# Paired Gelus, a period of three slots and weighted turns in a convolution and attention kernel

## The chip, the cores and the metric

The kernel runs on one NeuronCore of one Trainium2 chip. The metric is the device time of one execution in microseconds (us), as the median of several runs. Engines are named TensorE (PE in the profile, PEld for its weight loads), VectorE (DVE), ScalarE (ACT), GpSimd (POOL) and SyncE (SP, which issues the DMAs here).

## The reference

Four layers work on four images of 128 channels and 64 x 64 pixels in fp32. Layers 0 and 1 are where the change lies:

```python
# layer 0, on group-normalised x
feat = _gelu(_dwconv2d(x_adapted, conv1_w, conv1_b))
ca = feat.mean((2, 3))
ca = jax.nn.sigmoid(jnp.maximum(ca @ ca1_w.T, 0.0) @ ca2_w.T)
feat = feat * ca[:, :, None, None]
feat = _gelu(_dwconv2d(feat, conv2_w, conv2_b))
scores = jax.nn.sigmoid(jnp.einsum('bchw,oc->bohw', feat, head_w)[:, 0] + head_b[0])
pv = jnp.var(x_adapted, axis=1, ddof=1)
final_scores = 0.7 * scores + 0.3 * jax.nn.sigmoid(pv * 10.0)
sm = final_scores.reshape(B, Hp, PS, Wp, PS).mean((2, 4)).reshape(B, Hp * Wp)
idx = jnp.argsort(-sm, axis=1)
...
h = dA_t * h + dBx_t                      # a scan over 4096 positions, 256 x 16 states
...
# layer 1
x = x + _L1_conv_ref(_gn(x), L1_conv_weight, L1_conv_bias)      # a 3 x 3 convolution, 128 to 128 channels
```

In words: layer 0 scores the 4 x 4 patches of an image by two depthwise convolutions with exact Gelus and by the variance over channels, sorts the patches by score, sends the sorted pixels through a selective state-space scan and puts the result back in the old order. Layer 1 is a dense 3 x 3 convolution. Layer 2 is an attention with softmax and a mixture of experts, layer 3 a linear attention and another mixture. Layers 2 and 3 are not touched.

## The kernel before, in words

**Stages.** `layers01` has three stages. First `in_order(0)` prepares image 0 alone: group norm, first depthwise convolution, channel weights, second depthwise convolution with scores, sort, position encoding and layer norm, permutation. Then `scan` runs the state-space scans of the four images, one after the other, with other work beside them: `in_order(b + 1)` while image b is scanned, and, beside the last scan (image 3), `end` of images 2, 0 and 1, which puts sorted pixels back (`put_back`) and runs layer 1 (`convolve`). Last comes `end(3)` alone. Layers 2 and 3 follow.

**Chunks and slots.** An image of 4096 positions is cut in 8 chunks (`NCH`) of 512 (`CH`). For a chunk the scan has 8 state groups (`NG`) of four scans each; a group is two slots, so a chunk has 16 slots (`SLOTS`), a scan of an image 128. I count the slots of an image from 0 to 127: slot 66 is slot 2 of chunk 4. At the head of a group VectorE multiplies into `hs` (line 901); each slot then has two exponentials on ScalarE (line 908, "decay", in two PSUM banks), a flush of the work put off, two scans on VectorE (line 912), a carry copy and a product with the C row on GpSimd (lines 915 and 916). In odd slots TensorE adds the previous group into `y_ps` (`add`); in even slots, after the work beside it, it spreads the next B row (`b_ps`, `spread_b`), and SyncE loads the next C row (`c_sb`, `spread_c`). In the first slots of a chunk `enter` prepares the next chunk (`xc_ps`, Silu, `dbc`, `dt`), and `leave` finishes the last one. `gate` comes in slot 8.

**The order of the work.** In the scan stage all five engines run in the order in which the code issues (`tc.manual_schedule`); alone, before and after it, a scheduler may reorder. The work beside the scans consists of generators; one `next` is a turn. Beside scans 0 to 2 one turn is taken per slot, and all that is left in slot 111; beside scan 3 turns are taken from slot 8 at an even pace, 53 turns an end (`TURNS_END`), 159 turns in 120 slots. `staged(n, period, ...)` starts item c at turn c x period and runs one stage a turn; `together` and `chain` combine generators. The second depthwise convolution of chunk c is issued in slot 47 + 2c, the first one's in slot 27 + 2c.

What reads a result of TensorE is put off: `K.later` keeps it for the next `K.flush`, which is called in each slot between the exponentials and the scans, and between two turns of one slot. `K.bank` hands out the three PSUM banks that the work beside shares; when the bank due is still in use, it flushes at once:

```python
while self.count - self.banks in self.live:
    assert self.late
    self.flush()
```

`enter` holds a bank from slot 1 of a chunk until its Silus are issued, in the flush of slot 3 or in an earlier one that `K.bank` forces.

**What the change touches.** `first` (line 476) and `second` (line 530) are the depthwise convolutions of one chunk, `gauged` (line 539) sums squares and features over channels and takes a Tanh; `seconds` (line 557) schedules them. Before, Gelu reads PSUM for each chunk, adds the bias and, in `first`, accumulates the sum for the channel weights. Gelu and Exp need different activation tables, so that a Gelu beside the scans has a table load ahead of it and one behind. `put_back`, `convolve` and `end` (lines 955 to 1029) are the last stage's turns; `Common.__init__` and `same_block` make constants.

## Time and profile before

| what | value |
|---|---|
| median of 3 runs | 9885.43 us (9885.13 to 9886.97) |
| the profiled execution, its own time | 9881.09 us |
| its span, first to last instruction | 9879.3 us |
| mean granted clock of TensorE | 0.92 |
| preparation of image 0 and first entry | 0 to 236.8 us |
| scan of image 0, 1, 2 | 580.1, 582.0, 579.8 us |
| scan of image 3, with three ends | 656 us |
| end of image 3, alone | to some 2750 us |
| busy in scans 0 to 2, each | VectorE 509 to 511, TensorE 478 to 481, ScalarE 398 to 399, GpSimd 417 to 422 us |

How to read the page: busy time is the sum over an engine's instructions; the lines of tenths cut the span in 40 slices. In a list of groups the columns are line, engine, operation, tiles written and read, count, then busy us and mean ns, then the idle time of the engine just ahead of these instructions, with what ended it. In a timeline they are start, duration, engine, line, instruction, and in brackets the idle time before it and its releaser. Helpers hide lines: all matmuls through `mm` stand at line 91, all that is put off by `K.later` with its arguments at line 130.

### The profile page before, as it was taken

What the parts mean: (1) busy time and instruction counts of PE and PEld (TensorE: products, weight loads), DVE (VectorE), ACT (ScalarE), POOL (GpSimd) and SP (SyncE); (2) the same over time, 40 slices, a digit from 0 to 9 for tenths busy, and PEclk for the clock granted to TensorE, in tenths of its full rate; (3) what the DMA queues carried; (4) which work ended last, traced back from release to release, by engine and by line L of the source; (5) the groups of instructions that cost most, each with busy time, mean ns of one, the idle gap of its engine ahead of it and who ended that gap; (6) DMA issues with size and microseconds to landing.
All of it is one profiled execution on the core that took longest, in us unless ns stands there. A gap on an engine that the chain in (4) does not pass through costs nothing.

```text
span 9879.3 us, 187787 instructions
## 1 busy us (share of the span) xinstructions
PE 8736.1 (88%) x74074; PEld 3348.6 (34%) x74074; DVE 7220.5 (73%) x7877; ACT 7410.6 (75%) x10669; POOL 4802.8 (49%) x3175
## 2 busy tenths in 40 slices
PE   5888888888869999989999989999989999967776
PEld 2222222244523333333333333333333333333433
DVE  2889897988658888758888758888758888743463
ACT  3766767654359999879999879999879999841531
POOL 1677676765435555455555455555455555420000
PEclk8887878889979999989999989999989999988997
DMA  4524435223121221231111131211131211124004
GB/s 116 124 69 118 97 83 125 67 76 88 46 70 40 40 40 41 48 94 39 40 39 41 46 97 39 40 40 39 44 101 39 39 40 39 40 93 121 1 18 154
DMA packets 575731, 635.31 MB, mean 64 GB/s; under 512 B 113080, under 2 KB 369152, under 8 KB 573824
## 3 DMA queue, kind: packets, MB, share of 16 engines
q1 hardware_dynamic: 574848, 623.30, 25.6%
q8 instruction: 584, 9.57, 0.4%
q14 instruction: 299, 2.45, 0.1%
HBM read 446.84 MB, written 109.07 MB: 56 GB/s over the span
## 4 chain that ended last, share of the span: by engine, by line
PE 69%; DVE 10%; POOL 6%; ACT 5%; DMA 4%; issue 3%; SPq 2%; DVEq 0%; POOLq 0%; ACTq 0%
PE ctx_ps L91 27%; PE acc_ps L91 13%; PE score L91 11%; PE conv L91 4%; DVE hs L912 3%; POOL hs L916 3%; PE ln_xc L91 2%; PE y_ps L91 2%; DVE hs L901 2%; PE xc_ps L91 1%; DMA w<-in_L_ffn_weight 1%; PE ln_var L91 1%; PE b_ps L91 1%; PE hid_ps L91 1%; PE kv L91 1%
## 5 line engine op out<-in xcount | busy, mean ns | idle before, releaser
L1535 ACT ACTIVATE ex<-score 128x1024 f32<-128x1024 f32 x5120 | 4925.4, 1036 | 218.5 <-PE score L91 125.7
L91 PE MATMUL ctx_ps<-ex,qt 128*32 128x512 f32 x20480 | 2733.9, 606 | 19.9 <-DVE ctx L1469 19.9
L1484 POOL TENSOR_TENSOR folded<-ex 128x1024 f32<-128x1024 f32 x512 | 1224.2, 2391 | 2101.5 <-ACT ex L1535 1836.6
L1541 DVE STREAM_TRANSPOSE turned<-ex 128x1024 f32<-128x1024 f32 x1536 | 1885.8, 1228 | 329.1 <-ACT ex L1535 328.7
L1517 DVE STREAM_TRANSPOSE turned<-ex 128x1024 f32<-128x1024 f32 x1532 | 1842.4, 1203 | 0.0
L91 PE MATMUL acc_ps<-turned,turned_v 128*32 128x256 f32 x24576 | 1769.5, 379 | 3.1 <-POOL qt L1229 2.3
L912 DVE TENSOR_TENSOR_SCAN hs<-decay,carry,hs 128x512 f32<-128x512 f32 x1024 | 1245.7, 1266 | 193.6 <-ACT decay L908 180.1
L91 PE MATMUL score<-queries,keys 32*128 32x512 f32 x10240 | 1335.3, 497 | 44.0 <-POOL queries L1219 37.9
L91 PEld LDWEIGHTS acc_ps<-turned,turned_v 128*32 128x32 f32 x24576 | 800.9, 110 | 1476.5 <-issue 1323.8
L916 POOL TENSOR_TENSOR hs<-hs,c_sb 128x1024 f32<-128x1024 f32 x512 | 1207.3, 2358 | 81.4 <-DMA c_sb<-c_d 40.3
L908 ACT ACTIVATE decay<-dt,a_neg 128x512 f32<-128x512 f32 x1024 | 693.0, 689 | 662.5 <-DVE hs L912 653.3
L91 PEld LDWEIGHTS score<-queries,keys 32*128 32x128 f32 x10240 | 512.6, 182 | 1139.2 <-ACT ex L1535 780.9
L1347 POOL TENSOR_TENSOR turned_v<-v,quarter 128x1024 f32<-128x1024 f32 x256 | 612.4, 2393 | 265.7 <-PE acc_ps L91 225.0
L91 PE MATMUL y_ps<-hs,pair 128*64 128x512 f32 x2048 | 661.5, 773 | 33.6 <-POOL hs L916 33.6
L1485 POOL TENSOR_TENSOR quarters<-folded 128x512 f32<-128x512 f32 x512 | 657.7, 1285 | 40.2
L91 PEld LDWEIGHTS ctx_ps<-ex,qt 128*32 128x32 f32 x20480 | 406.4, 108 | 654.7 <-issue 598.7
L901 DVE TENSOR_TENSOR hs<-dtx,b_ps 128x2048 f32<-128x2048 f32 x256 | 580.1, 2266 | 55.9 <-PE b_ps L91 31.6
L91 PE MATMUL b_ps<-dbc,state 32*64 32x512 f32 x1024 | 343.2, 752 | 233.4 <-DVE hs L901 233.2
L1535 ACT ACTIVATION_READ_ACCUMULATOR ex<-score 128x1 f32 x2048 | 435.9, 213 | 0.0
L915 POOL COPY carry<-hs 128x2 f32<-128x2 f32 x512 | 98.1, 192 | 673.4 <-DVE hs L912 652.0
L1469 DVE COPY ctx<-ctx_ps 128x512 f32<-128x512 f32 x256 | 176.9, 691 | 329.3 <-PE ctx_ps L91 327.0
L1526 DVE TENSOR_REDUCE dacc<-quarters 128x2 f32<-128x512 f32 x508 | 327.1, 644 | 0.0
(371 smaller groups left out, 9016.1 us busy)
## 6 DMA issues: line engine op xcount, KB each, us to landing
c_sb<-c_d SPq DMA_DIRECT2D x512, 128.0 KB
queries<-head_d SPq DMA_DIRECT2D x1024, 64.0 KB
keys<-head_d SPq DMA_DIRECT2D x1024, 64.0 KB
under<-image_d SPq DMA_DIRECT2D x192, 264.0 KB
dt<-dt SPq DMA_DIRECT2D x128, 256.0 KB
dtx<-dtx SPq DMA_DIRECT2D x128, 256.0 KB
v<-value_d SPq DMA_DIRECT2D x1024, 32.0 KB
w<-in_L_ffn_weight SPq DMA_DIRECT2D x32, 1024.0 KB
```

Source lines behind the costliest of these rows:

```text
L91: self.nc.tensor.matmul(out, lhsT, rhs, start=start, stop=stop)
L901: nc.vector.tensor_tensor(hs, dtx2, bb.unsqueeze(1).to_broadcast([P, NQ, CH]), ALU.mult)
L908: nc.scalar.activation(ex, dt2[:, q, :], AF.Exp, scale=a_neg[:, q, g : g + 1])
L912: nc.vector.tensor_tensor_scan(hs[:, q, :], decays[q - 2 * i], hs[:, q, :], carry[:, g, q : q + 1], ALU.mult, ALU.add)
L916: nc.gpsimd.tensor_tensor(hs[:, two, :], hs[:, two, :], cs.unsqueeze(1).to_broadcast([P, 2, CH]), ALU.mult)
L1347: nc.gpsimd.tensor_tensor(t, v.unsqueeze(2).to_broadcast([P, 4 * BT, 4, HD]), quarter.unsqueeze(1).to_broadcast([P, 4 * BT, 4, HD]), ALU.mult,
L1484: nc.gpsimd.tensor_tensor(hs, exs[:, :, 0], exs[:, :, 1], ALU.add)
L1485: nc.gpsimd.tensor_tensor(qs, hs[:, :, 0 : CH // 2], hs[:, :, CH // 2 :], ALU.add)
L1517: nc.vector.transpose(*upright)
L1526: nc.vector.tensor_reduce(at, qs, AX.X, ALU.add)
L1535: nc.scalar.activation(ex, sps[p], AF.Exp, scale=scale, accum_out=sums[:, t : t + 1] if summed else None)
L1541: nc.vector.transpose(*upright)
```

## The change

In `first`, ScalarE takes the convolution out of PSUM with an Identity that adds the bias, chunk by chunk, and after every second chunk runs one Gelu in place over both, with one accumulated sum. `second` does the same in a buffer of two chunks, and Squares go to a buffer of two. The scores of both chunks of a pair are then taken in two turns of the later one (`gauged_first`, `gauged_second`), and a chunk of the second convolution begins every three turns instead of two. Chunk c's second convolution is then issued in slot 47 + 3c, the pairs' Gelus come in the flushes of slots 51, 57, 63 and 69, and what follows is seven turns later.

Beside the last scan a turn may carry a weight. The turns of group norm and the waits weigh 0.4, those of `put_back` 0.85, those of `convolve` 0.9, and turns are taken until their weights, not their number, reach what is due; an end counts as 40.3 (`SLOTS_END`).

To make room for the larger buffers, constants that are needed only to make others lie in a pool that is closed again, and two tiles of `put_back` share the place of tiles of the sort.

```diff
-        self.same4 = self.same_block("same4", 2)
-        self.same16 = self.same_block("same16", 4)
-        self.group_mean = pool.tile([P, P], F32, name="group_mean")
-        nc.vector.tensor_scalar(self.group_mean, self.same4, 0.25, None, ALU.mult)
+        with tc.tile_pool(reuse_waits="tile", name="temporary", bufs=1) as tmp:
+            self.same4 = self.same_block("same4", 2, tmp, tmp)
+            self.same16 = self.same_block("same16", 4, tmp, pool)
+            self.group_mean = pool.tile([P, P], F32, name="group_mean")
+            nc.vector.tensor_scalar(self.group_mean, self.same4, 0.25, None, ALU.mult)
...
-    TURNS_END = 53
+    SLOTS_END = 40.3
...
+        def weighted(weight, part):
+
+            while True:
+                try:
+                    next(part)
+                except StopIteration as over:
+                    return over.value
+                yield weight
...
-            fsum = small.tile([P, NCH], F32, name="fsum")
+            fsum = small.tile([P, NCH // 2], F32, name="fsum")
...
-                later(
-                    nc.scalar.activation,
-                    fp[:, 1 + 8 * c : 9 + 8 * c, 1 : HW + 1],
-                    rect(ps),
-                    AF.Gelu,
-                    bias=conv1_b,
-                    accum_out=fsum[:, c : c + 1],
-                )
+                later(nc.scalar.activation, fp[:, 1 + 8 * c : 9 + 8 * c, 1 : HW + 1], rect(ps), AF.Identity, bias=conv1_b)
+                if c % 2:
+                    at = fp[:, 8 * c - 7 : 8 * c + 9, 1 : HW + 1]
+                    later(nc.scalar.activation, at, at, AF.Gelu, accum_out=fsum[:, c // 2 : c // 2 + 1])
...
-                sq = squares[c] = work.tile([P, CH], F32, name="pv_sq", tag="ln_sq", bufs=1)
-                later(nc.scalar.activation, sq, mp, AF.Square)
+                if c % 2 == 0:
+                    squares[0] = work.tile([P, 2, CH], F32, name="pv_sq", tag="ln_sq", bufs=1)
+                    features[0] = work.tile([P, 2, CH], F32, name="f2", tag="rs", bufs=1)
+                sq, f2 = squares[0], features[0]
+                later(nc.scalar.activation, sq[:, c % 2], mp, AF.Square)
                 ps = convolved(unders.pop(c), deep2)
-                f2 = features[c] = work.tile([P, CH], F32, name="f2", tag="rs", bufs=1)
-                later(nc.scalar.activation, f2, ps, AF.Gelu, bias=conv2_b, scale=ca)
+                later(nc.scalar.activation, f2[:, c % 2], ps, AF.Identity, bias=conv2_b, scale=ca)
+                if c % 2:
+                    later(nc.scalar.activation, f2, f2, AF.Gelu)
+
+            def gauged_first(c):
+                if c % 2:
+                    gauged(c - 1)
+
+            def gauged_second(c):
+                if c % 2:
+                    gauged(c)
...
-                mm(ps[0:64], K.var1[:, 0:64], squares.pop(c))
-                mm(ps[64:128], head_bc, features.pop(c))
+                mm(ps[0:64], K.var1[:, 0:64], squares[0][:, c % 2])
+                mm(ps[64:128], head_bc, features[0][:, c % 2])
...
-            seconds = staged(NCH, 2, gather_second, None, None, second, None, gauged)
+            seconds = staged(NCH, 3, gather_second, None, None, second, None, gauged_first, gauged_second)
...
-                        begin, until, pace = 8, NCH * SLOTS, (NB - 1) * TURNS_END / (NCH * SLOTS - 8)
+                        begin, until, pace = 8, NCH * SLOTS, (NB - 1) * SLOTS_END / (NCH * SLOTS - 8)
...
-                            if next(beside, True):
+                            weight = next(beside, 0)
+                            if weight == 0:
                                 beside = None
-                            done += 1
+                            done += weight or 1
...
-                pi = small.tile([P, 256], F32, name=f"perm_inv{h}")
+                pi = small.tile([P, 256], F32, name=f"perm_inv{h}", tag=f"beats{h}")
...
-            scale = yield from K.groupnorm_scale(xb, xp, small, psum)
+            scale = yield from weighted(0.4, K.groupnorm_scale(xb, xp, small, psum))
...
-            yield from together(
-                staged(NCH, 1, lambda c: K.groupnorm_fill(xb, xp, scale, c)), chain(wait(3), staged(2 * NCH, 1.5, piece))
-            )
-            yield from wait(2)
+            fills = staged(NCH, 1, lambda c: K.groupnorm_fill(xb, xp, scale, c))
+            yield from weighted(0.9, together(fills, chain(wait(3), staged(2 * NCH, 1.5, piece))))
+            yield from weighted(0.4, wait(2))
...
-            yield from wait(2)
-            yield from put_back(xb, xq[:, 0:L], rank, work, psum)
+            yield from weighted(0.4, wait(2))
+            yield from weighted(0.85, put_back(xb, xq[:, 0:L], rank, work, psum))
```

More of the change, by code (lines that the diff above doesn't have):

```diff
@@ L66, in __init__, with shifted, same_block @@
         nc.vector.tensor_scalar(self.row[:, 1:2], self.row[:, 0:1], 128.0, None, ALU.add)
-        self.same4 = self.same_block("same4", 2)
-        self.same16 = self.same_block("same16", 4)
-        self.group_mean = pool.tile([P, P], F32, name="group_mean")
-        nc.vector.tensor_scalar(self.group_mean, self.same4, 0.25, None, ALU.mult)
-    def shifted(self, name, src, n, ops):
+        with tc.tile_pool(reuse_waits="tile", name="temporary", bufs=1) as tmp:
[3 more added lines that the diff above has]
+            nc.vector.tensor_scalar(self.group_mean, self.same4, 0.25, None, ALU.mult)
+    def shifted(self, name, src, n, ops, pool=None):
         nc = self.nc
-        ti = self.pool.tile([P, n], I32, name=name + "_i")
+        pool = pool or self.pool
+        ti = pool.tile([P, n], I32, name=name + "_i")
         nc.vector.tensor_scalar(ti, src, *ops)
-        tf = self.pool.tile([P, n], F32, name=name)
+        tf = pool.tile([P, n], F32, name=name)
         nc.vector.tensor_copy(tf, ti)
         return tf
-    def same_block(self, name, shift):
+    def same_block(self, name, shift, tmp, pool):
         nc = self.nc
-        r = self.shifted(name + "_r", self.row_i, 1, (shift, None, ALU.arith_shift_right))
-        c = self.shifted(name + "_c", self.col_i[:, 0:P], P, (shift, None, ALU.arith_shift_right))
-        t = self.pool.tile([P, P], F32, name=name)
+        r = self.shifted(name + "_r", self.row_i, 1, (shift, None, ALU.arith_shift_right), tmp)
+        c = self.shifted(name + "_c", self.col_i[:, 0:P], P, (shift, None, ALU.arith_shift_right), tmp)
+        t = pool.tile([P, P], F32, name=name)
         nc.vector.tensor_scalar(t, c, r, None, ALU.is_equal)
```

## The prediction

> **What bounds the kernel now.** First the page: no engine is full over the span, so the shares say little, and I went to the stage that the diff touches, layers 0 and 1, which end at about 2750 us of 9879.3. The lines of busy tenths show it as the first eleven slices, with VectorE at 8 or 9 in slices 2 to 11 and ScalarE at 6 or 7.
>
> ```profile
> DVE  2889897988658888758888758888758888743463
> ACT  3766767654359999879999879999879999841531
> ```
>
> Then the timeline of VectorE, from the first scan of each slot to that of the next. A slot is half a state group: an even slot has two scans, an odd slot two scans and the 2.26 us product of the next group (line 901). Undisturbed slots last 2.4 and 4.7 us in turn; a chunk of 16 slots lasts 62.2 us when nothing lies beside it (chunk 6 of batch 0, with the next chunk's entry in it). The chunks of batch 0 last 64.8, 71.1, 73.3, 89.0, 87.6, 69.8, 62.2, 62.4: 82 us above 8 x 62.2, alike in batches 1 and 2. The excess lies where the convolutions (chunks 1 to 3) and the position work (4, 5) run beside the scans. Batch 3 lasts 656 us, 159 above.
>
> The groups of VectorE and ScalarE in scans 0 to 2 (columns: busy us, mean ns, idle before and its releaser) name the wait:
>
> ```profile
> L912 DVE TENSOR_TENSOR_SCAN hs<-decay,carry,hs 128x512 f32<-128x512 f32 x769 | 934.5, 1265 | 172.0 <-ACT decay L908 161.4 <-DVE hs L901 0.9
> ...
> L908 ACT ACT_TABLE_LOAD x129 | 165.5, 1283 | 2.3
> L130 ACT ACT_TABLE_LOAD x99 | 127.0, 1283 | 23.4 <-PE conv L91 20.8
> ...
> L130 ACT ACTIVATE dt<-dtx 128x1024 f32<-128x1024 f32 x24 | 25.4, 1057 | 0.3
> ...
> L130 ACT ACTIVATE f<-conv,conv_b,ca 128x512 f32<-128x512 f32 x24 | 18.7, 777 | 0.3
> ...
> L130 ACT ACTIVATE fp<-conv,conv_b 128x512 f32<-128x512 f32 x24 | 16.5, 689 | 26.3 <-PE conv L91 26.1
> ```
>
> The scans wait 161 us in all, 54 a batch, for the exponentials ("decay"). One such wait, ScalarE's timeline in slot 48 and VectorE's beside it:
>
> ```profile
> 448.19 1.28 ACT L130 ACT_TABLE_LOAD   x1 [1.85 <-PE conv L91]
> 449.49 0.78 ACT L130 ACTIVATE f<-conv,conv_b,ca 128x512 f32<-128x512 f32 x1
> 450.28 1.28 ACT L908 ACT_TABLE_LOAD   x1
> 451.58 1.30 ACT L908 ACTIVATE decay<-dt,a_neg 128x512 f32<-128x512 f32 x2
> ```
>
> ```profile
> 452.30 2.46 DVE L912 TENSOR_TENSOR_SCAN hs<-decay,carry,hs 128x512 f32<-128x512 f32 x2 [3.92 <-ACT decay L908]
> ```
>
> ScalarE waits for the convolution, loads Gelu's table, runs Gelu, loads Exp's again; the exponentials of the odd slot are queued behind. That is 3.35 us of which 2.57 are loads, in an even slot, where the scans last only 2.4.
>
> Batch 3 is different: there TensorE is full. Rows of two stretches (chunk 5 of batch 3, chunk 6 of batch 0: us, PE, PEld, DVE, ACT, POOL busy, clock):
>
> ```profile
> 2388.50:2480.90 92.40, 82.03 (x318) 45.40 (x317) 71.78 (x65) 41.71 (x58) 50.32 (x36) 0.91 0.36 105
> 692.30:754.60 62.30, 50.75 (x139) 13.70 (x140) 59.47 (x46) 39.20 (x52) 46.80 (x36) 0.75 0.30 72
> ```
>
> **What the Trainium skill says.** "ScalarE: Activation LUTs", section "What ACT_TABLE_LOAD costs": a load of 1283 ns and a drain of 1380 for each switch. The trace has the 1283, but the next activation starts 1.30 us after the load's start (450.28, 451.58): I use 1.28. Same page, "Table sets: the hidden batching unit": cheap functions are in every set, exp shares one with tanh. The trace agrees: fills (Identity), Squares and Tanhs stand between exponentials with no load. "TensorE: Matmul & The Clock Gate", "What's actually happening": the array is throttled until it is busy. The trace agrees (mean clock 0.82 in scans 0 to 2; eight y_ps matmuls take 1.94 or 3.68 us): a sparser TensorE may be slower, a bound I keep for the range.
>
> **First convolution, part by part.** Per pair of chunks the change removes two Gelus (2 x 0.69), four loads and one accumulator read (192 ns in the same list), and adds two Identities (2 x 0.69, like the Gelu they replace) and a Gelu over 1024 (1.06, from the row of 1024 elements) with two loads. ScalarE: -2.57 - 0.19 + 1.06 = -1.7 us a pair. The flush slots are 28, 30, ... 42, as before. Their excess over 2.4 in batch 0 is 1.2, 7.3, 1.8, 0, 2.3, 4.0, 1.4, 2.3. Chunks 0, 2, 4, 6 keep only the Identity, whose 0.69 fits: 6.7 becomes 0.7. The odd ones gain 1.06 each, some of it under slack: +3.2. **Gain 3** a batch (bounds 0 and 7, four times 1.7).
>
> **Second convolution.** Chunk c comes at slot 47+3c (before: 47+2c). So Gelus fall in the flushes of slots 51, 57, 63, 69, all odd, where VectorE has the 2.26 us product to do as well. Old excess of slots 48 to 63 is 26.7 us. New, slot by slot: 48, Identity still behind the Sigmoid's load of the channel weights, 4.0 less (0.09 and one 1.28 load), 2.6; 53, as before, 2.0; 54, 0.5; 60, 0.9 (Tanh, Square, Identity, 2.05 us, and the wait for the convolution); the pairs' Gelus: 0.59 + 0.69 + 1.28 + 1.06 + 1.28 + 0.69 = 5.6 us against some 4.9 to the next product, 0.7 at 63 and 69, 0.4 at 57; 67, 0.5. Sum 8.3, **gain 18.4**. Position work is 7 slots later, an odd number, so the product with the centring matrix leaves the even slots, in which it stood ahead of the B spread (TensorE waits 15 us for "pos_xc" in batch 0): **gain 3** (0 to 8).
>
> **What the move collides with.** Only three PSUM banks serve all this. A fourth request in a slot, or a second one while the entry of the next chunk holds a bank (slots 1 and 2 of a chunk), flushes early. Slot 66 now has this, ScalarE and VectorE:
>
> ```profile
> 548.68 0.69 ACT L767 ACTIVATE xc<-xc_ps,conv1d_b 128x512 f32<-128x512 f32 x1 [1.75 <-PE xc_ps L91]
> 552.12 0.69 ACT L767 ACTIVATE xc<-xc_ps,conv1d_b 128x512 f32<-128x512 f32 x1 [2.75 <-PE xc_ps L91]
> ```
>
> ```profile
> 552.51 0.32 DVE L648 STREAM_TRANSPOSE ln_vt<-pos_var 128x128 f32<-128x128 f32 x1 [4.57 <-PE pos_var L91]
> 554.84 1.28 DVE L912 TENSOR_TENSOR_SCAN hs<-decay,carry,hs 128x512 f32<-128x512 f32 x1 [2.02 <-ACT decay L908]
> ```
>
> It costs 4.57 + 2.02 = 6.6 us, and goes, since centring moves to odd slots. In its place, counted by requests: slot 50 (entry and second convolution; chain Silu 12.2, Square, load, exponential 14.8 after the product, against 10.6: 4.2), 56 (gate and convolution, 1.8), 65 (2.0), 68 (1.5); and the sort's permutation moves from slots 88-97 to 95-104, into chunk 6's entry: 98 is a new slot 66 (6.6), 100 and 101 together 2.0. Seven flushes, 18.1, less 6.6: **loss 11.5**.
>
> A batch: -3 - 18.4 - 3 + 11.5 = -12.9; three: **-39**. In-order preparation takes 106 turns instead of 99, within the 112 slots, so nothing spills. Moved DMAs: gathers now alternate between even and odd slots on SP and have a slot or two more after the convolution that frees their buffer; nothing is charged (0 to -3).
>
> **Weighted ends.** An end has 53 turns before, 1.325 a slot. Now convolution turns weigh 0.9 (1.0075/0.9 = 1.12 a slot), put-back 0.85 (1.19), group norm and waits 0.4 (2.5). A piece is 65.03/16 = 4.06 us of TensorE at full clock (the undisturbed last end):
>
> ```profile
> 2677.32 65.03 PE L91 MATMUL conv<-xp,taps 128*128 128x256 f32 x288 [1.64 <-issue]
> ```
>
> A slot without it has 1.5 us (y_ps 1.94 and b_ps 1.07 a group). Two thirds of a piece a turn: 1.325 x 2.71 + 1.5 = 5.1 a slot before, 4.5 after; VectorE has 62.2/16 = 3.9 and 0.476 us a piece, 4.3. So TensorE exceeds it by 0.8 x 20 slots before and 0.2 to 0.3 x 24 after: 9 an image, 27 for three. I take 16: the second image's run now holds chunk 4's entry (14 us of TensorE) whole, and each run begins with three turns without pieces. Group norm packed at 2.5 a slot puts aggregate and its product in one slot (VectorE waits 0.58 + 0.68) and the offset just ahead of the first fill: 2 us an end, +6. Put-back is bound by VectorE's adds either way. **-10** (-27 to +10).
>
> **Alone, ahead of the scans.** There are no Gelu loads to save (Tanh and Gelu follow each other without one); TensorE waits for Identity and Gelu once a pair, 2.05 against 2 x 0.96, with one squares product (0.87) no longer under it: +1 a pair, +4 (0 to +8). Temporary constants: the first small loads may wait for VectorE's set-up, which ends at 8.7: +2 (0 to +8).
>
> **Sum.** -39 - 10 + 6 = -43: 9881.1 (the profiled execution: span 9879.3 and 1.8 around it) becomes 9838; the median of runs, 9885.4, is 4.3 above: **9842**.
>
> **Rivals.** (1) Large gain: flushes cost little (2.6 becomes 1), ends give 27: -39 - 17 - 3 x 11 = -89, 9796. For it, 161 us of scans waiting; against, slot 66. Chance 0.13. (2) Washed out: the seven flushes cost 4.5 each (24.9 a batch net, 75 in three) and take back the gains of 3 x 24.4 + 10 - 6 = 77; or TensorE, with gaps of a slot more between convolutions, falls to half clock there: 9883. Chance 0.18. (3) Slower: early flushes decide. If each of the seven costs what slot 66 costs, 6.6, the loss is 7 x 6.6 - 6.6 = 39.6 a batch, 119, against the same 77: 9927. From 5.6 each on it is 0.2% slower. For it, the one measured; against, four of the seven hold only short copies or Silus. Chance 0.14, with (4). (4) Identity needs a table too and no load goes: fills between exponentials show none. It would leave 9885 plus the added Gelus. Forecast (9810 to 9865): 0.55.
>
> 0.2%, about 20 us, is what a measurement of this kernel can tell from no change. Faster: 0.55 + 0.13 = 0.68; within, case (2), 0.18; slower 0.14. Range 9780 to 9905: it leaves out the slower case and the best of the large gain.
>
> **To be seen after.** 129 + 99 loads of lines 908 and 130 in scans 0 to 2 fall by 48; the wait of scans for decay falls from 161 to 110 or less; slot 66 near 2.4, slots 50 and 98 near 7; chunk 6 of batches 0 to 2 above 70 us, chunk 3 near 75; VectorE's "xb<-conv" waits for TensorE (43 us) fall to 30. Wrong: chunks 3 to 6 longer in sum than 309 us, or batch 3 above 656.

## The result, and the profile after

| | before | after |
|---|---|---|
| median of six runs each, us | 9886.2 | 9943.2 |
| ratio (95% interval) | | 1.006 (1.0047 to 1.0073) |
| profiled span, us | 9879.3 | 9942.6 |
| preparation of image 0 | 236.8 | 228.3 |
| scans of images 0, 1, 2 | 580.1, 582.0, 579.8 | 593.8, 597.4, 597.3 |
| scan of image 3 | 656.3 | 672.4 |
| the rest (last end, layers 2 and 3) | 7244 | 7253 |

The change makes the kernel slower by 0.6%; the forecast was 0.4% faster. Of the 63 us between the spans, scans 0 to 2 have +46.6 (forecast -39), image 3 +16.1 (-10), the preparation -8.5 (+6) and the untouched rest +9. That rest differs by some 30 us between the profiles of this study, so it carries no meaning. A stage that an edit leaves alone repeats within some 5 us, save that chunk 2 of images 1 and 2 took anything from 72 to 79 us; the sum of three scans is therefore sure to some 10 us only.

By pairs of chunks of an image: chunks 1 and 2, with the first convolution, +5 to +7 (144.4 to 151.1 in image 0); chunks 3 and 4, with the second, -12 to -16 (176.6 to 160.3); chunks 5 and 6, where sort and position work now lie, +23 to +24 (132.0 to 155.2).

The busy tenths of the changed kernel's page: VectorE has no 9 left in slices 4, 6 and 8, and ScalarE has 6 in slices 2, 5 and 7 where it had 7: both do as much or less in more time.

```profile
DVE  2888887887748888858888858888758888744463
ACT  3666656654439999969999979999979999841531
```

The groups of scans 0 to 2 in the changed kernel (line, engine, operation, tiles, count, then busy us and mean ns, then idle time just ahead and what ended it). Line 931 is the scan, 927 the exponentials, 920 the product, 132 what is put off:

```profile
L931 DVE TENSOR_TENSOR_SCAN hs<-decay,carry,hs 128x512 f32<-128x512 f32 x769 | 932.2, 1264 | 181.9 <-ACT decay L927 172.6
...
L920 DVE TENSOR_TENSOR hs<-dtx,b_ps 128x2048 f32<-128x2048 f32 x192 | 434.8, 2265 | 44.1 <-PE b_ps L93 24.1 <-POOL dtx L132 8.1 <-issue 7.7
...
L927 ACT ACT_TABLE_LOAD x102 | 130.9, 1283 | 1.8
L132 ACT ACT_TABLE_LOAD x75 | 96.2, 1283 | 2.5
...
L132 ACT ACTIVATE f<-conv,conv_b,ca 128x512 f32<-128x512 f32 x24 | 18.6, 775 | 29.9 <-PE conv L93 29.7
L132 ACT ACTIVATE fp<-conv,conv_b 128x512 f32<-128x512 f32 x24 | 16.4, 682 | 50.9 <-PE conv L93 50.9
L132 ACT ACTIVATE fp<-fp 128x1024 f32<-128x1024 f32 x12 | 12.7, 1059 | 0.1
```

The loads did go: 129 + 99 became 102 + 75, 51 fewer, near the 48 forecast. The forecast's signs of being wrong came true: chunks 3 to 6 take 315 to 319 us in sum (309 was the limit), image 3 takes 672 (656). But the scans wait 172.6 us for decay instead of 161.4, not 110. ScalarE's waits for the convolution grew from 46.9 (26.1 at fp, 20.8 at the loads of the f Gelus) to 80.6, and the product waits 44.1 instead of 13.2. Removing work from ScalarE exposed a wait that had lain under it. On VectorE, whose busy time is the same, 31 us of the new idle time stand ahead of the product, 10 ahead of the scans and 14 ahead of a copy of the permutation (perm_s, 0.7 to 14.3), with some 8 less elsewhere.

Slot 30 of image 0 shows how. ScalarE before the change, where the Gelu's load is issued ahead of the wait for the convolution:

```profile
348.31 1.28 ACT L130 ACT_TABLE_LOAD   x1
350.64 0.69 ACT L130 ACTIVATE fp<-conv,conv_b 128x512 f32<-128x512 f32 x1 [1.04 <-PE conv L91]
```

All engines in the same slot of the changed kernel (weight loads and some lines left out):

```profile
352.22 4.88 PE L93 MATMUL conv<-under,deep 96*32 96x512 f32 x24 [2.76 <-DMA under<-image_d]
...
354.55 1.57 SPq L889 DMA_DIRECT2D c_sb<-c_d  x2
...
357.17 0.69 ACT L132 ACTIVATE fp<-conv,conv_b 128x512 f32<-128x512 f32 x1 [9.26 <-PE conv L93]
357.87 1.28 ACT L132 ACT_TABLE_LOAD   x1
...
359.17 1.06 ACT L132 ACTIVATE fp<-fp 128x1024 f32<-128x1024 f32 x1
360.13 0.19 ACT L132 ACTIVATION_READ_ACCUMULATOR fp<-fp 128x1 f32 x1
360.33 1.28 ACT L927 ACT_TABLE_LOAD   x1
...
361.63 1.30 ACT L927 ACTIVATE decay<-dt,a_neg 128x512 f32<-128x512 f32 x2
...
362.35 2.46 DVE L931 TENSOR_TENSOR_SCAN hs<-decay,carry,hs 128x512 f32<-128x512 f32 x2 [10.43 <-ACT decay L927]
```

The convolution waits for its gathered input (`under`), runs at the lower pace (4.88 us for its 24 matmuls; 2.78 in most slots), and only then come Identity, load, Gelu, accumulator and load one behind the other, 4.4 us; none of it is under the wait. In image 1, slots 30, 34, 38 and 42 take 12.9, 4.3, 9.2 and 5.7 us (9.1, 2.4, 6.4 and 4.7 before), slots 36 and 40 3.4 and 2.4 (4.7 and 3.8).

### The profile page after: what moved, and what is told of

The parts are those of the page before. It is cut to its first block, busy times and chain, and to the rows that moved or that the text cites. A ratio compares the mean times of both kernels' runs of the same rounds, so it can differ in the third digit from the quotient of the medians.

```text
span 9942.6 us, 187727 instructions
## 1 busy us (share of the span) xinstructions
PE 8745.6 (88%) x74074; PEld 3354.8 (34%) x74074; DVE 7212.4 (73%) x7877; ACT 7380.0 (74%) x10637; POOL 4796.4 (48%) x3175
## 4 chain that ended last, share of the span: by engine, by line
PE 69%; DVE 9%; POOL 7%; DMA 5%; ACT 5%; issue 4%; SPq 2%; DVEq 0%; POOLq 0%; ACTq 0%
PE ctx_ps L93 26%; PE acc_ps L93 13%; PE score L93 11%; PE conv L93 4%; POOL hs L935 3%; DVE hs L931 2%; PE y_ps L93 2%; PE xc_ps L93 2%; PE ln_xc L93 1%; DVE hs L920 1%; DMA under<-image_d 1%; PE ln_var L93 1%; DMA w<-in_L_ffn_weight 1%; PE b_ps L93 1%; PE perm_p L93 1%
```

## The experiments

Unless said otherwise an edit is made in the kernel before. "Scans" is the sum of scans 0 to 2 in the profile, 1741.9 before and 1788.5 after.

### The three parts alone

**e1_first**: only the first convolution's pairs (the edits of `first` and `fsum` above).

> The kernel before with the paired Gelu of the first depthwise convolution alone. Theory Q (order of the queues): before the change the table load ahead of each of these Gelus was hidden in ScalarE's wait for TensorE, so a pair removes little and puts Identity, load, Gelu over 1024 and load in one row behind the convolution. Scans 0 to 2 then become 6 us longer each (chunks 1 and 2), about 9902 us. Rival R (loads count): ScalarE has 1.7 us less a pair, scans 3 to 7 us shorter each, about 9870.

Measured: 9895.8 us, 1.0009 (1.0001 to 1.0018); scans 1760.8 (+18.9), nearly all of it (17.8) in chunks 1 and 2. **e2_second**: only the second convolution, with its period of three and the constants.

> The changed kernel without the paired first convolution and without the weights: pairs and a period of three slots in the second convolution, with what makes room for them. Theory Q: chunks 3 and 4 gain 13 us a scan together, chunks 5 and 6 lose 24, because the position work and the permutation, seven slots later, meet the entry of the next chunk: scans 0 to 2 longer by 9 to 11 us each, the preparation of image 0 shorter by some 6 us, about 9910. Rival R: the loss in chunks 5 and 6 comes from the paired first convolution or other parts, and this part alone is faster, about 9865.

Measured: 9916.3, 1.0031 (1.0019 to 1.0042); scans 1784.9 (+43). **e3_ends**: only the weights.

> The kernel before with the weighted turns of the ends alone. Theory Q: group norm packed at 2.5 turns a slot flushes the entry's Silus, Relus and Lns ahead of the next exponentials and costs 25 us in three ends, the late load of the sorted pixels 10; the thinner convolution turns give 15 back: scan 3 at 672 us instead of 656, about 9902. Rival R: scan 3 gets shorter by the 10 to 16 us of the convolution turns, about 9873.

Measured: 9903.7, 1.0014 (1.0007 to 1.0021); image 3 takes 671.0 (+14.7), chunks 1, 3 and 6 of it 82.9, 104.3 and 86.4 instead of 74.0, 88.2 and 75.8. Each part alone is a loss, the first only just, and the three ratios make up 0.54 of the 0.60%. In the scans the first two do not simply add: 18.9 and 43 make 62, where the change has 46.6.

### The second convolution: pairs, period, shift

**e4_later7**: no pairs, the old period, but all that follows the second convolution seven slots later.

```diff
+            for _ in range(7):
+                next(tail, None)
+                yield
             perm = []
```

> The kernel before with seven empty turns ahead of the sort and the position work: the shift alone, no Gelu paired, period still two. Theory Q: chunks 4 to 6 lose 15 to 18 us a scan against before, scans 0 to 2 longer by about 50 us in sum, about 9935. Rival R: a shift by itself costs nothing, it moves the same work into slots of the same kind, within 10 us of 9886.

Measured: 9911.7, 1.0022 (1.0013 to 1.0032); scans 1772.1 (+30). In the three images together chunk 4 gains 42 us and chunks 5 and 6 lose 74; in the changed kernel chunks 3 and 4 gain 41 and chunks 5 and 6 lose 71, so that the shift alone gives nearly all of what the second convolution does there. **e5_later1**: the same with one turn.

> The kernel before with one empty turn ahead of the sort and the position work, so that this work moves by one slot from even to odd slots and still ends ahead of slot 2 of chunk 6 but for one request. Theory Q (what the shift loses is the meeting with the next chunk's entry in chunks 5 and 6; what it gains, 14 us in chunk 4, is the odd parity and the early flush of slot 66): chunk 4 near 74 us instead of 87, chunks 5 and 6 near 70 and 62, scans 0 to 2 shorter by 8 to 13 us each, about 9855. Rival R (the entries of chunks 4 and 5 are alike, the gain of chunk 4 is only work moved out of it): chunks 4 to 6 in sum as before, 219 us, about 9887.

Measured: 9882.9, 0.9995 (0.9986 to 1.0003); scans 1750.8, of which 8.5 us more lie in chunk 2, which the edit does not touch; chunk 4 is only some 1.5 us shorter, and chunks 4 to 7 take 5 more in sum. Parity alone is worth nothing. **e6_period3**: the period of three, no pairs.

```diff
-staged(NCH, 2, gather_second, None, None, second, None, gauged)
+staged(NCH, 3, gather_second, None, None, second, None, gauged)
```

> The kernel before with a period of three slots in the second convolution and one Gelu a chunk as before (no pairs): what comes later is seven turns late, as in the run with seven empty turns. Theory Q: the spacing alone gives little, since every second Gelu still falls in an even flush and the convolutions of even slots now stand ahead of the B spread: chunk 3 some 80 us (89 before), chunk 4 up by what was moved there, scans 0 to 2 in sum 1770 to 1790 against 1772 with the empty turns. Rival R: the pairs are what costs in the second convolution; without them the sum is below 1755.

Measured: 9923.6, 1.0036 (1.0023 to 1.0048); scans 1785.1. With the pairs (e2_second) they take 1784.9: **pairing the second Gelus brings nothing in the scans**, the shift costs 30 and the period 13 more, all in chunks 3 and 4. The 13 are near the noise (the ratios of e4_later7 and e6_period3, 1.0022 and 1.0036, have intervals that overlap), and pairs at a period of two were not tried.

**e8_later7_two_rs**: e4_later7 with two buffers for features and layer-norm scales, in the room of the temporary constants.

```diff
-tag="rs", bufs=1
+tag="rs", bufs=2
```

> The kernel with seven empty turns, with two buffers instead of one for the scale rows (and the second features), which ScalarE fills and GpSimd reads, in the room that the change makes. Theory Q: with one buffer ScalarE's copy waits for GpSimd, which is behind with the entry's three products (7.7 us in slot 92 of the changed kernel), and the exponentials wait behind the copy; with two, chunk 5 falls from 79 to 72 to 75 us, scans 0 to 2 from 1772 to about 1755. Rival R: GpSimd's backlog reaches TensorE and VectorE anyway, chunk 5 stays within 2 us of 79.

Measured: 9902.3, 1.0012 (1.0006 to 1.0019); scans 1774.2, no better, as rival R had it: ln_rs waits 16.3 us for xn instead of 37.5, but VectorE then waits 33.2 ahead of perm_s instead of 19.2. The preparation of image 0 is 13 us shorter than in e4_later7 (222.7), for two reasons that the trace shows. The eight copies of ln_rs in it span 13.4 us instead of 17.9. And in every run with the temporary constants SyncE issues the load of the image (`xb`) at the start; the first convolution begins at 39.0 to 40.6 us, in all runs without them at 44.5 to 47.6. The load, before and after the change:

```profile
19.39 1.85 SPq L388 DMA_DIRECT2D xb<-in_x  x4
```

```profile
1.19 1.84 SPq L390 DMA_DIRECT2D xb<-in_x  x4
```

**e11_later16**: e4_later7 with 16 turns, a whole chunk.

> The kernel before with 16 empty turns (a whole chunk of slots) ahead of the sort and the position work, so that these stand where they stood in a chunk, one chunk later; four turns are left to slot 111. Theory R (what the shift by 7 cost was its new place beside the entry of the next chunk, whose products fill GpSimd's queue): the chunks 4 and 5 of before, 88 and 70 us, come back as chunks 5 and 6, chunk 4 is near 64, scans 0 to 2 take 1738 to 1755, time 9882 to 9898. Rival S (any shift costs, since the work before it and after it no longer overlaps): 1765 or more, as with 7 turns (1772), time 9905 or more.

Measured: 9908.7, 1.0018 (1.0011 to 1.0024); scans 1773.3. The chunks 87.6 and 69.8 of image 0 come back as 90.1 and 73.4 one chunk later. Two rows of scans 0 to 2, before and in e4_later7:

```profile
L706 DVE COPY perm_s<-perm_t 128x512 f32<-128x512 f32 x24 | 16.1, 672 | 0.7 <-PE perm_t L702 0.7
...
L672 ACT COPY ln_rs<-pos_rs 128x512 f32<-128x512 f32 x24 | 13.9, 580 | 38.2 <-PE pos_rs L668 24.2 <-POOL xn L677 13.9
```


```profile
L710 DVE COPY perm_s<-perm_t 128x512 f32<-128x512 f32 x24 | 16.4, 683 | 19.2 <-PE perm_t L706 19.2
...
L676 ACT COPY ln_rs<-pos_rs 128x512 f32<-128x512 f32 x24 | 14.0, 584 | 37.5 <-POOL xn L681 37.5
```

With the shift by seven, ScalarE idles as long ahead of ln_rs as before, but all of it ends with GpSimd's xn; new on VectorE is the wait of 19.2 us ahead of perm_s. With 16 turns both are nearly back (3.0 for perm_s, 13.9 for xn), so the place beside the next chunk's entry is what changed them. The total did not come back: the product's wait for b_ps is 31.8 instead of 12.4. In image 1, slot 81 takes 10.4 (slot 65 before: 7.6), with b_ps behind pos_xc, which waits 5.26 us for GpSimd; slot 111, with four turns in it, takes 8.3 (slot 95 before: 5.1), and slot 117 6.7 (slot 101: 4.7). Some 8 of the 31 us lie in chunks 0 to 3, which the edit does not touch. So the place beside the entry is supported as the reason of the two waits, but that a shift by a chunk is free is refuted, and the two waits cannot be the whole cost of a shift.

### What the loads are worth

**e9_gelu_late**: no pairs; each Gelu one slot later, from an even slot to an odd one.

```diff
-                later(
+                K.much_later(
                     nc.scalar.activation,
                     fp[:, 1 + 8 * c : 9 + 8 * c, 1 : HW + 1],
...
-                later(nc.scalar.activation, f2, ps, AF.Gelu, bias=conv2_b, scale=ca)
+                K.much_later(nc.scalar.activation, f2, ps, AF.Gelu, bias=conv2_b, scale=ca)
```

> The kernel before, with nothing paired and nothing moved except that each Gelu of both depthwise convolutions is put off by one slot, from the flush of the even slot after its convolution to that of the odd slot behind it; the same Gelus and the same table loads remain. Theory E (what counts is in which slot a Gelu's loads lie: behind the exponentials of an odd slot some 4.7 - 2 x 0.65 = 3.4 us are free before the next group's first scan, in an even slot 1.1, and a Gelu with two loads is 3.35): the even slots 28 to 42 and 48 to 62 fall near 2.4, the odd ones grow by 0 to 0.7 each, chunks 1 to 3 lose 10 to 25 us an image, scans 0 to 2 end at 1665 to 1710 instead of 1742, the time is 9810 to 9855. Theory F (the number of loads and activations is what the scans pay, wherever they stand): scans 0 to 2 within 10 us of 1742, time 9878 to 9896. A bank of PSUM is held a slot longer: if that forces early flushes, the time may be above 9896.

Measured: 9870.0, 0.9980 (0.9972 to 0.9987); scans 1733.9. Two rows of its scans:

```profile
L912 DVE TENSOR_TENSOR_SCAN hs<-decay,carry,hs 128x512 f32<-128x512 f32 x769 | 932.7, 1265 | 71.9 <-ACT decay L908 61.3 <-DVE hs L901 0.5
...
L901 DVE TENSOR_TENSOR hs<-dtx,b_ps 128x2048 f32<-128x2048 f32 x192 | 435.5, 2268 | 80.4 <-PE b_ps L91 80.2 <-issue 0.2
```

The even slots 28 to 42 fell to 2.4 to 3.5 us, and the wait for decay by 100 us, as theory E had it. But the product's wait for b_ps rose by 68, and the scans took only 8 us less: in image 1 the odd slots 31, 33 and 35 take 8.2, 10.3 and 10.3 (4.7, 5.9 and 5.4 before), slot 53 13.8 (7.2). The wait changed its name. **e10_pair_late**: e1_first with the pair's Gelu a slot later.

```diff
-                    later(nc.scalar.activation, at, at, AF.Gelu,
+                    later(later, nc.scalar.activation, at, at, AF.Gelu,
```

> As e1_first (Identity for each chunk, one Gelu for two chunks in the first depthwise convolution), but the Gelu of a pair is issued one slot later, in an odd slot. Work on every engine is that of e1_first. Theory E: the even slots keep only the Identity (2.4 to 3.4 us) and the odd slots 31, 35, 39, 43 hold 1.28 + 1.06 + 0.19 + 1.28 = 3.8 us against 3.4 free; scans 0 to 2 fall from e1_first's 1761 to 1715 to 1735, time 9860 to 9880. Theory F: as e1_first, 1761 and 9896. If the waits of TensorE for the convolution's input decide, as in slot 30, some 1750.

Measured: 9899.9, 1.0006 (0.9998 to 1.0014); scans 1760.5, as e1_first's 1760.8. The sum speaks against theory E, the slots do not: slots 28 to 43, where the pairs lie, take 80.3, 83.0 and 80.3 us in the three images (e1_first 86.3, 87.0 and 86.1; before 81.6, 80.3 and 80.0), so the loss of the pairs is gone there. It comes back in slot 48, with 11.0, 11.5 and 9.0 us (e1_first 7.4, 6.3 and 6.2): the first gather of the second convolution reads what the last pair's Gelu, now a slot later, has stored. The convolution in slot 48 of image 1, in e1_first and here:

```profile
1036.55 2.78 PE L91 MATMUL conv<-under,deep 96*32 96x512 f32 x24 [0.49 <-DMA under<-image_d]
```

```profile
1032.61 5.35 PE L91 MATMUL conv<-under,deep 96*32 96x512 f32 x24 [2.24 <-DMA under<-image_d]
```

Even so a late pair only draws level with the kernel before. **e13_no_loads** bounds what the loads can be worth in this order of the work:

```diff
-                    AF.Gelu,
+                    AF.Tanh,
...
-                later(nc.scalar.activation, f2, ps, AF.Gelu,
+                later(nc.scalar.activation, f2, ps, AF.Tanh,
```

> The kernel before, with a Tanh in the place of each Gelu of both depthwise convolutions; the Gelu is left out, so that the scores are others. Tanh stood between exponentials without a load in the kernel before, so the 32 loads of an image (41 us of ScalarE) go and all else stays. It bounds what any pairing of Gelus can bring. Theory L (the loads hold the scans up): slots 28 to 43 fall from 80 to about 70 us an image, 48 to 63 from 88 to about 70, scans 0 to 2 from 1742 to 1660 or less. Theory T (the order on TensorE holds them up: y_ps, 3.7 us at half clock, the convolution, 3.8 to 4.7, and the spread of the B row, 1.1, in a row are 8.5 to 9.5 us for a group of 7.1): slots 28 to 43 stay at 75 to 82, only the second convolution gains, scans 0 to 2 take 1705 to 1740.

Measured: 9864.5, 0.9979 (0.9971 to 0.9987); scans 1728.3. Rows of its scans 0 to 2:

```profile
L912 DVE TENSOR_TENSOR_SCAN hs<-decay,carry,hs 128x512 f32<-128x512 f32 x769 | 933.3, 1264 | 131.8 <-ACT decay L908 120.3 <-DVE hs L901 0.9
...
L901 DVE TENSOR_TENSOR hs<-dtx,b_ps 128x2048 f32<-128x2048 f32 x192 | 434.8, 2264 | 35.3 <-PE b_ps L91 35.3
L908 ACT ACT_TABLE_LOAD x84 | 107.8, 1283 | 1.5
L130 ACT ACT_TABLE_LOAD x51 | 65.4, 1283 | 2.1
...
L130 ACT ACTIVATE f<-conv,conv_b,ca 128x512 f32<-128x512 f32 x24 | 18.6, 777 | 52.0 <-PE conv L91 52.0
L130 ACT ACTIVATE fp<-conv,conv_b 128x512 f32<-128x512 f32 x24 | 16.4, 684 | 62.6 <-PE conv L91 62.6
```

93 loads, 119 us of ScalarE, are gone, and the scans are 13.6 us shorter (the whole time 21, between 13 and 29). The waits for the convolution went from 46.9 to 114.6. Slot 30 of image 1 (TensorE, ScalarE, GpSimd) shows what is left, with no load in it:

```profile
940.68 5.20 PE L91 MATMUL conv<-under,deep 96*32 96x512 f32 x24 [2.55 <-DMA under<-image_d]
...
945.95 0.69 ACT L130 ACTIVATE fp<-conv,conv_b 128x512 f32<-128x512 f32 x1 [9.37 <-PE conv L91]
...
946.74 2.36 POOL L916 TENSOR_TENSOR hs<-hs,c_sb 128x1024 f32<-128x1024 f32 x1 [4.75 <-DMA c_sb<-c_d]
```

The gathered input comes late, and so does the C row (`c_sb`), which SyncE issues at 943.11 us, behind a gather (940.31). **e14_third_conv** shortens the convolution and keeps the loads.

```diff
-                for kx in range(3):
+                for kx in range(1):
...
-                            stop=kx == 2,
+                            stop=kx == 0,
```

> The kernel before, with one of the three column shifts of both depthwise convolutions (8 matmuls of 24 a chunk; two thirds of the taps are left out, so that the scores are others). Gelus and loads stay. Theory T: 2.5 us less of TensorE in each group with a convolution, slots 28 to 43 fall from 80 to 66 to 73 an image, 48 to 63 from 88 to about 78; scans 0 to 2 from 1742 to 1660 to 1700. Theory L: ScalarE still waits less for the convolution in slots such as 30, but the loads stay in the way; 1715 or more.

Measured: 9841.8, 0.9954 (0.9937 to 0.9970), but 24 of these us are in the preparation (213.1); the scans take 1729.6. Two thirds of the convolution are thus worth no more than all of its loads. That does not refute theory T, for two reasons. The convolution is shorter than the theory took it: 24 matmuls take 2.78 us in most slots, not 3.8 to 4.7. And TensorE slowed down. Scans 0 to 2 before and here (us, PE, PEld, DVE, ACT, POOL busy, granted clock, DMA share, GB/s):

```profile
236.80:1978.70 1741.90, 1437.93 (x5024) 420.95 (x5026) 1530.37 (x1232) 1195.34 (x1595) 1259.73 (x960) 0.82 0.40 98
```

```profile
213.10:1942.70 1729.60, 1398.09 (x4255) 405.62 (x4256) 1530.82 (x1231) 1196.61 (x1595) 1259.98 (x960) 0.79 0.40 99
```

The convolution's matmuls fell from 142.2 to 59.9 us, but TensorE's busy time only by 40; in slots 28 to 43 the granted clock is 0.70 to 0.74, where it was 0.84 to 0.89. In these slots, 81.6, 80.3 and 80.0 us before in the three images, 78.0, 74.6 and 78.1 are left without loads, 78.9 in each with the short convolution, 81.0 to 82.7 with late Gelus.

**e12_late_two_rs**: e9_gelu_late with e8_later7_two_rs's buffers.

> e9_gelu_late with two buffers for the features and the scales of the layer norm (tag rs) in the room that the change's temporary constants give. Theory: e9_gelu_late's time less the 14 us by which two such buffers shortened the preparation of image 0 in e8_later7_two_rs: preparation near 223, time 9795 to 9845. Rival: the gain of the preparation came from the empty turns there; then as e9_gelu_late.

Measured: 9865.1, 0.9977 (0.9968 to 0.9987); preparation 224.7, scans 1738.5. The preparation came out as expected, the time did not: it cannot be told from e9_gelu_late's.

### The ends

**e7_gn_unpacked**: e3_ends with the group norm at weight 0.8 (44.3 slots an end).

> The kernel before with weighted ends in which the turns of group norm weigh 0.8 instead of 0.4 (an end then counts 44.3), so that they come at 1.38 a slot. Theory Q: the packed group norm is what the weights lose by; without it the thinner convolution turns show: scan 3 at 640 to 650 us (before 656, weighted 671), about 9880. Rival R: the loss is the early load of the next image's pixels and the convolution turns themselves; scan 3 stays at 665 or more, about 9897.

Measured: 9898.8, 1.0007 (0.9999 to 1.0016); image 3 takes 666.4. Chunks 1 and 6 are mended (76.0, 78.7), chunk 3 is not (97.1), and most of the gain of chunk 2 is gone (88.1; 81.8 in e3_ends, 91.0 before). **e15_ends_wait1**: e3_ends with one number changed and the total adapted.

```diff
-    SLOTS_END = 40.3
+    SLOTS_END = 41.5
...
-            yield from weighted(0.4, wait(2))
+            yield from weighted(1.0, wait(2))
             yield from weighted(0.85, put_back(xb, xq[:, 0:L], rank, work, psum))
```

> e3_ends with the two waiting turns ahead of put_back at weight 1 instead of 0.4 (and 41.5 slots an end instead of 40.3), so that the sorted pixels have two slots to arrive instead of less than one. Theory W (the 8 us in which put_back waits for its pixels in chunk 3 come from the short wait): chunk 3 of image 3 falls from 104 to 92 to 96, the scan of image 3 from 671 to 660 to 664. Rival: the load itself starts late, behind the last image's end on its buffer; then 671 within 3.

Measured: 9868.6, 0.9982 (0.9974 to 0.9991); image 3 takes 643.5, 27 less than e3_ends and 13 less than before. Chunk 3 fell to 92.3, as theory W had it, but so did chunks 1 and 6 (75.6, 78.3), which it did not foresee. **e16_ends_gn_wait1**: e15_ends_wait1 with the group norm at 0.8.

> As e15_ends_wait1, with the group norm at weight 0.8 as in e7_gn_unpacked (45.5 slots an end). Theory: packing (5 us) and the short wait (8 us) are the cost of the ends and the rest is the thinner convolution, of which little is left at this pace; 652 to 660 for image 3, time within 0.1% of before. Rival: something else of the weights costs; 665 or more.

Measured: 9894.1, 1.0007 (0.9999 to 1.0016); image 3 takes 660.1, at the edge of what was expected, but the reason falls: e15_ends_wait1, packed, takes 643.5. The packed group norm is thus no cost by itself: with the longer wait it is the better one.

**e18_after_wait1**: the changed kernel with the two numbers of e15_ends_wait1.

> The changed kernel, with the two waiting turns ahead of put_back at weight 1 and 41.5 slots an end, as in e15_ends_wait1. If the ends are a cause of their own: the scan of image 3 falls from 672 to 643 to 648 and the time from 9943 to 9912 to 9920, still 0.3% above before, which is then the part of the two convolutions. If what image 3 lost is bound up with the changed preparation: 660 or more, 9930 or more.

Measured: 9908.3, 1.0026 (1.0018 to 1.0034); image 3 falls from 672.4 to 644.8, scans 0 to 2 stay (1788.6). The ends are a cause of their own. Chunk 1 of image 3 tells how, first in the changed kernel (87.0 us; DVE, PE and ACT, lines left out):

```profile
2114.09 0.38 PE L93 MATMUL gn_mp<-gn_mv,group_mean 128*128 128x1 f32 x2 [2.03 <-DVE gn_mv L175]
...
2119.91 3.78 PE L93 MATMUL dt_ps<-dbc,dt_projT 8*128 8x512 f32 x4
2122.08 0.69 ACT L812 ACTIVATE sp_u<-dt_ps,dt_b 128x512 f32<-128x512 f32 x1 [8.20 <-PE dt_ps L93]
...
2125.61 2.46 DVE L931 TENSOR_TENSOR_SCAN hs<-decay,carry,hs 128x512 f32<-128x512 f32 x2 [5.67 <-ACT decay L927]
...
2126.20 1.28 ACT L206 ACT_TABLE_LOAD   x1
...
2127.77 1.28 ACT L132 ACT_TABLE_LOAD   x1
...
2130.20 1.28 ACT L132 ACT_TABLE_LOAD   x1
...
2133.28 1.28 ACT L927 ACT_TABLE_LOAD   x1
...
2135.29 2.46 DVE L931 TENSOR_TENSOR_SCAN hs<-decay,carry,hs 128x512 f32<-128x512 f32 x2 [6.97 <-ACT decay L927]
```

and in e18_after_wait1 (75.6 us):

```profile
2112.92 1.98 PE L93 MATMUL dt_ps<-dbc,dt_projT 8*128 8x512 f32 x4
2114.14 0.69 ACT L812 ACTIVATE sp_u<-dt_ps,dt_b 128x512 f32<-128x512 f32 x1 [0.86 <-PE dt_ps L93]
...
2118.78 0.58 PE L93 MATMUL gn_mp<-gn_mv,group_mean 128*128 128x1 f32 x2 [3.88 <-DVE gn_mv L175]
```

With the short wait the group norm's product (gn_mp) is ahead of the entry's dt_ps on TensorE, dt_ps then runs late and at the lower pace, and one slot (22) holds the tables of Sqrt, Exp, Ln and Exp again. With the longer wait dt_ps goes first, three loads do, and slots 21 and 22 take 5.3 and 5.1 us instead of 10.3 and 9.7. In chunk 3 the pixels' load shows: slots 50 and 51 take 7.3 and 16.3 us after the change, with put_back's first transpose waiting 8.03 us for the pixels; before they take 2.4 and 8.2, in e15_ends_wait1 2.4 and 8.6.

```profile
2268.51 0.45 PE L991 MATMUL perm_t<-ident,xq 128*128 128x128 f32 x1 [8.03 <-DMA xq<-y_d]
```

### The parts that help, together

**e17_late_and_ends**: e12_late_two_rs with e15_ends_wait1's ends.

> e12_late_two_rs (both Gelus one slot later, no pairs, period of two slots, two buffers for the features) with the ends of e15_ends_wait1. If the parts add up: 0.9977 x 0.9982 = 0.9959 of before, some 9847 us; preparation 223 to 226, scans 0 to 2 1732 to 1740, image 3 643 to 648. If not: 9860 or more.

Measured: 9854.8, 0.9968 (0.9956 to 0.9980); preparation 229.4, scans 1732.7, image 3 645.1. The two parts together (0.9959) lie within the interval; only the preparation missed its range. It beats both kernels: 0.3% below the one before, 0.9% below the changed one.

## Why the prediction was wrong, point by point

**What bounds the kernel** named the wait, 161 us of scans for decay, and gave the loads as its reason from one slot (48) in which ScalarE waited for the convolution ahead of the load. That slot is like 17 of the 24 Gelus of the second convolution, whose load waits 0.4 to 2.2 us for it. The 24 loads of the first convolution never waited (0.02 us ahead of each): they ran beside the convolution. This step failed, that the loads are what the scans wait for, and the two next rest on it: with no loads at all 13.6 us of the three scans went (e13_no_loads), while the forecast took 3 x 21.4 = 64 from half of the Gelus.

**First convolution**: gain 3 an image was forecast, a loss of 6 measured (e1_first: 18.9 / 3). The slots that keep only an Identity gained 4.8 in image 1, where 6 was forecast. The failed term is "the odd ones gain 1.06 each", 3.2 in all: it put the pair's Gelu and loads in the place of a Gelu's own, whose first load had run beside the convolution. Now all 4.4 us come behind the wait for it: slots 30, 34, 38 and 42 of image 1 grew by 3.8, 1.9, 2.8 and 1.0, 9.5 in all.

**Second convolution, centring, and what the move collides with.** Of the terms, those that lie in chunks 3 and 4 make -18.5 an image (18.4 for the second Gelus, 3 for the centring and 6.6 for slot 66, less 9.5 for early flushes); measured -13.8. Those in chunks 5 and 6 make +8.6; measured +23.6. So most of the error lies in the slots behind. Pairing gives nothing of the gain (e2_second and e6_period3 are alike in the scans), and the seven turns alone do nearly the same to both pairs of chunks (e4_later7): the saving of 18.4 is work moved away. The centring's gain of 3 is not there; e5_later1 makes that step alone. Slot 66 fell to 2.4 and slot 98 took 7.3 to 9.0, as forecast; slot 50 took 5.2 instead of 6.6. The loss of 11.5 was right in kind, too small in size, and looked for in one resource only, PSUM banks. In chunk 6 the banks are most of it: slots 98, 100 and 101, where VectorE now waits ahead of perm_s, grew by 9.7 to 11.3 an image (8.6 forecast), out of 12 to 14. What it left out is chunk 5, for which nothing was forecast and which lost 9 to 11: slots 81, 82, 85, 89 and 92 grew by 1.6 to 4.4 each, in e4_later7 as in the changed kernel. Which of their waits are the cause is not shown. ScalarE's wait ahead of ln_rs for GpSimd is not the cost by itself, since more than half of it went in e8_later7_two_rs and the scans were no shorter. Of the rivals, the slower case (3) had the right sign, from dearer collisions, but its mechanism, seven flushes at 6.6 us, is not what the slots show.

**Moved DMAs**, put at 0 to -3, cost time: the convolutions wait longer for their gathered input, first before, then after the change.

```profile
L91 PE MATMUL conv<-under,deep 96*32 96x512 f32 x1152 | 142.2, 629 | 13.9 <-DMA under<-image_d 10.5 <-ACT fp L130 3.3
```

```profile
L93 PE MATMUL conv<-under,deep 96*32 96x512 f32 x1152 | 158.9, 691 | 41.6 <-DMA under<-image_d 27.7 <-ACT sz L132 13.1 <-ACT xc L786 0.6
```

The new waits are in slots 56 and 63, 4.4 and 5.0 us in each image. Slot 63 takes 10.4 where the forecast had 5.4, with b_ps behind the convolution.

**Weighted ends, -10**: the thinned convolution gained 14 in the three chunks that hold nothing else (2, 4 and 7), near its term of 16, and VectorE's waits for it fell from 43 to 23, below the 30 forecast. The group norm's +6 was mis-sized: chunks 1 and 6, where two of the three stand, lost 23. The put-back was put at nothing: slots 50 and 51 lost 13 to the late pixels. Shown is that the weight of the two waiting turns, with the total that goes with it, decides (e15_ends_wait1, e18_after_wait1: 27 us both times), not the packing that the forecast priced; that it does so through the order of gn_mp and dt_ps on TensorE and the late pixels is read from the timelines, not isolated.

**Alone, +6**: -8.5. The temporary constants were priced at +2, for small loads that wait for VectorE. They did wait (the first is issued at 10.5 us instead of 0.7), but that let the image's load go first, and the first convolution began 4.8 us earlier. This was luck for the forecast, whose sum the term made better.

**Open.** Why the period of three costs 13 us over the shift, if it does, and how the 30 of the shift split: two readings (GpSimd's products, b_ps behind pos_xc) are each supported by waits, neither was taken away by itself. Also open is what would shorten slots 28 to 43 below 75 to 78 us; the late `under` and c_sb are what is left to see, and an earlier gather was not tried.

## What to carry to other kernels

A wait that a profile puts down to one engine may be the last of several: before you price the removal of work there, ask what that engine would wait for next, and look whether the work had lain under a wait already. Where engines run in one written order beside each other, a shift of any piece by a turn or two may cost or gain more than the work it saves (27 us here from the weight of two turns), so that a change in a schedule is to be tried at several offsets before it is judged. Take the whole suspected cost away once, even with another function in its place: with no loads at all, and the order of the work as it was, the scans were 13.6 us shorter, so the forecast's 64 could not be there. And when the sum of a run stays the same, look at the slots before you drop the theory: in e10_pair_late a gain of 16 us was there and was lost again elsewhere.

## What the runs showed of the hardware

A table load that stands ahead of an activation that waits for TensorE can run during that wait (348.31, with the Gelu at 350.64 waiting another 1.04 us); it then costs nothing there. In "ScalarE: Activation LUTs" of the Trainium skill, "What ACT_TABLE_LOAD costs" prices every switch of tables at the 1283 ns of the load and a drain of some 1380 ns more; the traces agree for the 1283 ns, but 93 fewer loads shortened the scans by only 0.15 us each. A late transfer came with a second delay on TensorE: in scans 0 to 2 before and after the change, each convolution that waited 2.6 to 5.1 us for its input then took 4.75 to 5.35 us, most others 2.78. Less work for TensorE was in part paid back: with 82 us of convolution left out its busy time fell by 40, at a granted clock of 0.79 instead of 0.82 (e14_third_conv).
